# A fused graph-attention layer on one core: batch 0's self_feat by seven block products in the setup, partial sums in place

## The chip, the cores and the metric

The kernel runs on one core of a Trainium2 chip. The core has TensorE (matmuls, in the profile PE, and its weight loads PEld), VectorE (DVE), ScalarE (ACT), GpSimd (POOL) and SyncE (SP), which here only issues DMAs. Every engine works through its own instructions in order and waits on semaphores for the others. Matmuls write into PSUM, eight banks of 512 float32 for each of 128 partitions; VectorE and ScalarE read results from there. The metric is the device time in microseconds, as a median of several executions.

## What is computed

For 16 batches of 512 rows and 512 features (all float32):

```
q_exp     = 0 where a row of v sums to 0, else q[batch]
self_feat = concat(v, q_exp) @ W_self.T + b_self
output    = self_feat
for d in 0, 1:                       # both directions of the adjacency
    kv   = self_feat[:, :20]
    qh   = self_feat @ Wq[d].T + bq[d]          # 16 heads of 32
    kh   = kv @ Wk[d].T + bk[d]
    aff  = qh . kh / sqrt(32), masked by adj, plus a label bias
    out += softmax(aff) @ kv, each head through Wout[d], plus bout[d]
result    = v + relu(output)
```

The part that the change concerns is `self_feat`, a product of 512 x 512 by 512 x 512 for each batch, to which the q term is added (`nz`, the flags of rows that do not sum to zero, times `qw`, the q part of the product). The kernel holds it transposed: features on partitions, rows along the free dimension, in a tile `sf` of four chunks of 128 features. The first 20 rows (`NG`) come out of the setup already (`kvn`) and are copied in by `new_self`; the other 492 make two halves of 246 rows (`HN`).

## The kernel before, in words

There is a setup and a loop over batches with four tiles of 128 rows each (`nt`). All order is written out by hand (`manual_schedule`): instructions reach each engine's queue in the order of the program text.

**The setup** loads weights, computes the first 20 rows for all batches, and then works in 22 *bursts* (n = 0 to 21, function `keys`). A burst is eight matmuls into four PSUM banks (two tiles of the pool `ps_s`, which has just two), and these are copied out half by ScalarE (line 684) and half by VectorE (line 686) into a staging tile `st`, which SP then writes to DRAM for later batches. The next burst uses the same two tiles, so it has to wait for both copies. The stretch between two bursts is a *gap*. To fill gaps, the list `plan` names for each burst from n = 4 on what TensorE does behind it: `v` and `w` are steps of the value projection (`values`), `c` the bias scores, `n` the row flags of a batch (`row_flags`), and `s` a step of batch 0's self_feat (`self_step`: four matmuls). The fillers use four banks of the pool `ps_acc`.

**Batch 0's self_feat** is computed before in the plain way: `self_feat` runs for each pair of output chunks f and half h 32 matmuls of 32 output features and 236 or 256 rows, and `self_copy` adds the q term on VectorE on the way to `sf`. Three of the four (f, h) lie in gaps of the setup; the fourth, (1, 1), stands in the loop, at `nt == 1` of batch 0 between the first and the second tile's scores (line 864).

**From batch 1 on** self_feat is computed by seven block products instead of eight (a scheme of Strassen's kind, with four sums of weights, `weight_sums`, and four sums of x blocks for each batch, `x_sum`, both on GpSimd). `product(b, n)` is one of the seven: 16 matmuls with 246 columns. Products 1, 6, 7 and 4 accumulate one after the other into two banks `ps_a`; product 2 has the bank `ps_d`; products 5 and 3 accumulate in `ps_c`. Between the products VectorE takes out what stands in `ps_a` so far: `partial` adds the q term and writes a tile `u`, and `joined` adds a `u` to `ps_d` or `ps_c` and writes the block of `sf`. A product that adds to a bank has to wait until the `partial` or `joined` that reads the bank is through. These products for batch b + 1 run during batch b: products 1, 2 at its tile 2, 6, 7, 5 at its tile 3, and 4, 3 at tile 0 of batch b + 1.

**A tile of the loop**: `scores` (64 matmuls, line 353) into a `ps_s` tile, `weigh` on VectorE (add the mask `full`, which `full_add` makes on GpSimd; maximum; subtract), `expo` on ScalarE, `normal` (row sums on VectorE, scaling on GpSimd), `turn` (a transpose on VectorE). At tile 2 of the next batch, `attend` multiplies the weights with the value blocks `vd`, and `finish` and `residual` make the output. For batch 0 the value blocks are put together in DRAM by DMAs on SP (`clear_blocks`, `blocks`, `load_values`) during its own loop.

Of the kernel before, what the change touches and what calls it, by code (L numbers as in the profile page):

```python
# [13 lines left out]
P = 128  # L14
# [4 lines left out]
def gat_kernel(  # L19
# [71 lines left out]
    adds, fulls, wts, outs, held, sf_ps, conds, prods = {}, {}, {}, [], [None] * 3, {}, {}, {}  # L91
    sums, parts, us, done = {}, {}, {}, {}
# [98 lines left out]
    def self_feat(b, f, h, parts=((0, range(C)), (1, range(C)))):  # L191


        lo, hi = max(NG, h * N // 2), (h + 1) * N // 2
        for i, ks in parts:
            if (i, ks[0]) == (0, 0):
                if (f, h) == (0, 0):
                    new_self(b)
                held[0] = bank(f"ps_sf{b}_{f}{h}", 3 if (f, h) == (1, 1) else None)
            for k in ks:  # L200
                for a in range(HL):
                    nc.tensor.matmul(  # L202
                        held[0][bass.ts(a, R), i * N // 2 : i * N // 2 + hi - lo],
                        ws_v[:, k, bass.ds((2 * f + i) * P + a * R, R)], xs[b][:, k, lo:hi],
                        start=(k == 0), stop=(k == C - 1),
                    )
            if (i, ks[-1]) == (1, C - 1):
                sf_ps[b, f, h] = held[0]

    def self_copy(b, f, h):  # L210

        lo, hi = max(NG, h * N // 2), (h + 1) * N // 2
        ps = sf_ps.pop((b, f, h))
        for i in range(2):
            nc.vector.scalar_tensor_tensor(
                sfs[b][:, 2 * f + i, lo:hi], nzs[b][:, lo:hi], qw[:, 2 * f + i, b : b + 1],
                ps[:, i * N // 2 : i * N // 2 + hi - lo], ALU.mult, ALU.add,
            )

# [15 lines left out]
    def x_sum(b, n):  # L235

        t = sums[b, n] = xsum.tile([P, 2, HN], F32, tag=f"t{n}", name=f"t{b}_{n}")
# [8 lines left out]
    def product(b, n):  # L246
# [11 lines left out]
        if n == 1:  # L258
            parts[b, "a"] = [bank(f"ps_a{b}_{i}", i) for i in range(2)]
        if n == 2:  # L260
            parts[b, "d"] = bank(f"ps_d{b}", 2)
        if n == 5:
            parts[b, "c"] = bank(f"ps_c{b}", 3)
# [17 lines left out]
    def partial(b, n, f, l, to=None):  # L281

        if to is None:
            to = us[b, n] = xsum.tile([P, 2, HN], F32, tag=f"u{n}", name=f"u{b}_{n}")
        for i in range(2):
            done["partial"] = nc.vector.scalar_tensor_tensor(  # L286
                to[:, i], nzs[b][:, half(l)], qw[:, 2 * f + i, b : b + 1], parts[b, "a"][i][:, :HN],
                ALU.mult, ALU.add,
            )
# [4 lines left out]
    def joined(b, n, key, f, l):  # L294

        nc.vector.tensor_add(
            block(b, f, l), parts[b, key][:, : 2 * HN].rearrange("p (i n) -> p i n", i=2), us.pop((b, n))
# [155 lines left out]
    with tc.tile_pool(name="setup", bufs=1) as sp, tc.tile_pool(name="ps_acc", bufs=4, space=PSUM) as acc["pool"]:  # L453
# [157 lines left out]
        with tc.tile_pool(name="setup_g", bufs=4) as sg:  # L611
# [85 lines left out]
            def self_step(b, f, h, i, k):  # L697
                self_feat(b, f, h, ((i, (k,)),))
                if (i, k) == (1, C - 1):
                    self_copy(b, f, h)  # L700
# [6 lines left out]
                "s": [  # L707
                    (self_step, (0, f, h, i, k)) for f, h in ((0, 0), (1, 0), (0, 1))
                    for i in range(2) for k in range(C)
                ],  # L710
# [3 lines left out]
            plan = "bvv vv vv ccw vv ns ssss sssw vv vv ssss ssss vv vv nww ssss ssss".split()  # L714
# [13 lines left out]
            for n, runs in enumerate(bursts):  # L728
# [16 lines left out]
                if n == 10:  # L745
                    mask_sum(0, 0)
                    load_cq(0)
                if n == 11:
                    row_sums(1)
                if n == 13:  # L750
                    weight_sums()
# [17 lines left out]
    with tc.manual_schedule():  # L769
# [11 lines left out]
        for b in range(B):  # L781
# [7 lines left out]
            for nt in range(NT):  # L789
# [22 lines left out]
                if nt == 0:  # L812
# [4 lines left out]
                    else:  # L817
# [5 lines left out]
                        partial(b, 4, 1, 0, block(b, 1, 0))  # L823
# [222 lines left out]
```

## Time and profile before

| | us |
|---|---|
| median of three executions | 591.52 (590.48 to 591.87) |
| profiled execution, device time | 593.27 |
| its span, first to last instruction | 591.5 |
| TensorE busy | 578.7 |
| VectorE busy | 492.3 |
| ScalarE busy | 395.6 |
| GpSimd busy | 384.2 |
| mean granted TensorE clock | 0.995 |

The profile is one execution, recorded by the hardware. A line such as `L202 PE MATMUL ps_sf<-x,ws_v` names the line of the kernel, the engine, the operation, and the tile written and those read. In a timeline a line begins with the start in us from the first instruction and the duration; `xN` counts merged records (every matmul of this kernel leaves two). A bracket at the end says how long the engine stood idle just before and what ended that. The ends of matmuls are modelled: consecutive groups overlap by some 0.1 to 0.2 us, so the length of a group is read from its start to the start of the next.

### The profile page before, as it was taken

The page shows a single profiled execution, that of the slowest core. Times are in us where ns is not written, and L with a number is a line of the kernel's source. Part 1 is how long each engine was busy: PE and PEld are TensorE (multiplying, and loading weights), DVE is VectorE, ACT ScalarE, POOL GpSimd, SP SyncE. Part 2 cuts the span into 40 slices and gives each one's busy share as a digit, 9 for nine tenths or more (in the row PEclk, how much of TensorE's full clock was granted, in tenths as well). Part 3 has the DMA queues.
Part 4 walks back from the last instruction along what each step waited for, and adds up shares of the span by engine and source line. Part 5 has one row for each costly group of instructions (what it writes and reads, how often), then busy time and mean ns, then how long its engine had stood idle before and what let it go on. Part 6 is the DMA issues. An engine that isn't in the chain of part 4 may idle for free.

```text
span 591.5 us, 30038 instructions
## 1 busy us (share of the span) xinstructions
PE 578.7 (98%) x13180; PEld 439.7 (74%) x13180; DVE 492.3 (83%) x785; ACT 395.6 (67%) x1162; POOL 384.2 (65%) x351
## 2 busy tenths in 40 slices
PE   8999999999999999999999999999999999999994
PEld 6654547888978687787878787788787878787882
DVE  0495565889898888999999999888989898989896
ACT  1234644587877677768686868677787877777661
POOL 2315663638677675758686777675858677776774
PEclk9999999999999999999999999999999999999997
DMA  8998999857848485767676766757585748582503
GB/s 294 385 406 299 332 376 329 257 126 199 223 154 229 155 236 148 206 168 209 184 208 163 223 173 202 171 181 208 164 217 170 216 149 232 158 238 85 167 13 142
DMA packets 98129, 124.10 MB, mean 210 GB/s; under 512 B 19952, under 2 KB 70160, under 8 KB 95952
## 3 DMA queue, kind: packets, MB, share of 16 engines
q1 hardware_dynamic: 96752, 120.31, 67.1%
q8 instruction: 103, 1.69, 1.2%
q0 software_dynamic: 672, 1.36, 1.0%
q10 hardware_dynamic: 576, 0.53, 0.3%
q14 instruction: 26, 0.21, 0.1%
HBM read 82.30 MB, written 40.24 MB: 207 GB/s over the span
## 4 chain that ended last, share of the span: by engine, by line
PE 94%; DVE 3%; DMA 1%; issue 1%; ACT 0%; POOL 0%; SPq 0%; DVEq 0%; POOLq 0%; ACTq 0%
PE ps_s L353 44%; PE ps_a L279 17%; PE ps_c L279 8%; PE ps_o L426 6%; PE ps_d L279 4%; PE ps_v L644 3%; PE ps_k L581 3%; PE ps_sf L202 2%; DMA ws_q<-in_wsT 1%; PE ps_kv L532 1%; DVE o L435 0%; PE ps_nz L186 0%; DVE wt L415 0%; DVE ps_s L371 0%; DVE sm L406 0%
## 5 line engine op out<-in xcount | busy, mean ns | idle before, releaser
L353 PEld LDWEIGHTS ps_s<-g,sf 128*32 128x32 f32 x8192 | 264.0, 110 | 19.8 <-issue 12.2
L353 PE MATMUL ps_s<-g,sf 128*32 128x152 f32 x8192 | 277.3, 293 | 0.5 <-ACT st L684 0.5
L334 ACT COPY both<-add 32x80 f32<-32x80 f32 x512 | 130.9, 256 | 54.8 <-DVE add L325 49.0
L408 POOL TENSOR_TENSOR s<-s,sm 128x640 f32<-128x640 f32 x63 | 80.3, 1275 | 98.0 <-DVE sm L407 98.0
L341 POOL TENSOR_TENSOR full<-cq,both 128x640 f32<-128x640 f32 x64 | 100.1, 1565 | 30.3 <-issue 24.3
L314 ACT ACTIVATE prod<-adj,wb_sb 128x80 f32<-128x80 int32 x330 | 112.5, 432 | 0.0
L380 ACT ACTIVATE s<-s 128x640 f32<-128x640 f32 x63 | 46.5, 738 | 69.4 <-DVE s L375 69.0
L444 POOL TENSOR_TENSOR o<-o,x 128x512 f32<-128x512 f32 x60 | 75.9, 1285 | 0.0
L367 DVE TENSOR_TENSOR full<-ps_s,full 128x608 f32<-128x608 f32 x63 | 49.1, 779 | 32.1 <-PE ps_s L353 26.6
L406 DVE TENSOR_REDUCE sm<-s 128x32 f32<-128x640 f32 x63 | 50.9, 808 | 8.8 <-ACT s L380 8.6
L279 PE MATMUL ps_a<-t,ws_s 128*32 128x246 f32 x960 | 55.5, 370 | 0.0
L371 DVE TENSOR_REDUCE ps_s<-full 128x32 f32<-128x640 f32 x63 | 52.2, 828 | 2.2
L415 DVE STREAM_TRANSPOSE wt<-s 128x640 f32<-128x640 f32 x63 | 52.8, 839 | 0.1
L375 DVE TENSOR_TENSOR s<-full,ps_s 128x640 f32<-128x640 f32 x63 | 51.6, 818 | 1.1
L426 PE MATMUL ps_o<-wt,vd 32*32 32x512 f32 (+5 forms) x816 | 40.8, 581 | 3.7 <-DVE wt L400 2.0
L279 PEld LDWEIGHTS ps_a<-t,ws_s 128*32 128x32 f32 x960 | 32.2, 110 | 15.5
L325 DVE TENSOR_REDUCE add<-prod 128x80 f32<-128x960 f32 x32 | 36.8, 1150 | 6.3 <-ACT prod L314 4.4
L244 POOL TENSOR_TENSOR t<-x 128x492 f32<-128x492 f32 x30 | 34.4, 1148 | 10.1 <-DVE full L367 5.2
L439 ACT ACTIVATE o<-o,bo 128x512 f32<-128x512 f32 x60 | 38.2, 708 | 0.6 <-POOL biased L881 0.6
L435 DVE TENSOR_TENSOR o<-ps_o,sf 128x512 f32<-128x512 f32 x60 | 36.8, 672 | 1.0 <-PE ps_o L426 1.0
L286 DVE SCALAR_TENSOR_TENSOR u<-nz,qw,ps_a 128x246 f32<-128x246 f32 x90 | 36.6, 449 | 0.0
L244 POOL TENSOR_TENSOR t<-x,t 128x492 f32<-128x492 f32 x30 | 34.4, 1147 | 1.2
(238 smaller groups left out, 722.7 us busy)
## 6 DMA issues: line engine op xcount, KB each, us to landing
g_d<-st SPq DMA_DIRECT2D x16, 1064.0 KB, 5.9
g<-g_d SPq DMA_DIRECT2D x28, 608.0 KB, 5.2
out_T<-o SPq DMA_DIRECT2D x60, 256.0 KB, 4.7
xn<-in_xn SPq DMA_DIRECT2D x28, 512.0 KB, 3.6
x<-in_xT SPq DMA_DIRECT2D x28, 512.0 KB, 4.3
adj<-in_adj SPq DMA_DIRECT2D x32, 440.0 KB, 5.0
nz<-nz_d SPq DMA_DIRECT2D x14, 256.0 KB, 4.0
wk<-in_wkT SPq DMA_DIRECT2D x2, 1024.0 KB, 8.0
```

Of the source, the lines that this page charges most:

```text
L244: nc.gpsimd.tensor_sub(t, one, two)
L279: nc.tensor.matmul(to, lhs, x[:, k], start=start, stop=stop, skip_group_check=n != 2)
L314: nc.scalar.activation(p[:, :, l], a[:, :, l], AF.Identity, scale=wb_sb[:, l : l + 1])
L334: nc.scalar.copy(adds[b, h][bass.ts(a, R), :, g], add[r].rearrange("p (t m) -> p t m", t=2))
L341: nc.gpsimd.tensor_add(f, cqs[b].unsqueeze(1).to_broadcast(shape), adds[b, nt // 2][:, nt % 2].unsqueeze(2).to_broadcast(shape),)
L353: nc.tensor.matmul(bank[bass.ts(a, R), bass.ts(j, WD // HL)], sfs[b][:, k, bass.ds(nt * P + (2 * g + j) * R, R)], keys[:, k, a], start=(k ...
L371: nc.vector.tensor_reduce(mx, f, AX.X, ALU.max)
L375: nc.vector.tensor_sub(s, f, mx.unsqueeze(3).to_broadcast(full))
L408: done["normal"] = nc.gpsimd.tensor_mul(s, s, sm.unsqueeze(3).to_broadcast(full))
L415: nc.vector.transpose(wts[b][:, nt], s.rearrange("p a h m -> p (a h m)"))
L426: nc.tensor.matmul(banks[a][bass.ds(at // 2 * DH, n * DH)].rearrange("p (t n) -> p t n", n=32), vd[r, bass.ds(at * DH, n * DH)], wt[r, :, ...
L444: nc.gpsimd.tensor_add(o[:, c], o[:, c], xs[b][:, c])
```

## The change

Batch 0 gets its self_feat by the seven block products too.

- `self_feat` and `self_copy` are gone, and with them the 96 matmuls in gaps and the 32 matmuls in the loop at tile 1 of batch 0.
- The last seven gaps (n = 14 to 20) get one product each, in the order 1, 2, 6, 7, 5, 4, 3. Ahead of a product in the same gap stand, on VectorE: a partial ahead of 2, 7 and 4, a join ahead of 6 and 3; behind product 3 the last partial and the last join.
- The other fillers move up into n = 4 to 13; `row_sums(1)` and `weight_sums` move to n = 9, and at n = 11 the four x sums of batch 0 are made on GpSimd, into a tile of the `sf` pool.
- For all batches the partials are written straight into the block of `sf` and the join adds in place; the tiles `u` are gone. So `new_self` of the next batch moves from tile 3 to tile 2, ahead of that tile's exponential on ScalarE.
- In the setup the banks of the products come from the setup's own pool of four.

```diff
@@ x_sum
-        t = sums[b, n] = xsum.tile([P, 2, HN], F32, tag=f"t{n}", name=f"t{b}_{n}")
+        if b > 0:
+            t = xsum.tile([P, 2, HN], F32, tag=f"t{n}", name=f"t{b}_{n}")
+        else:
+            if n == 1:
+                held[0] = sfp.tile([P, C, N], F32, tag="sf", name="t0")
+            t = held[0][:, n - 1, : 2 * HN].rearrange("p (k n) -> p k n", k=2)
+        sums[b, n] = t
@@ product
-            parts[b, "a"] = [bank(f"ps_a{b}_{i}", i) for i in range(2)]
+            parts[b, "a"] = [bank(f"ps_a{b}_{i}", i if b else None) for i in range(2)]
...
@@ partial, joined
-    def partial(b, n, f, l, to=None):
-        if to is None:
-            to = us[b, n] = xsum.tile([P, 2, HN], F32, tag=f"u{n}", name=f"u{b}_{n}")
+    def partial(b, f, l):
+        to = block(b, f, l)
...
-    def joined(b, n, key, f, l):
+    def joined(b, key, f, l):
         nc.vector.tensor_add(
-            block(b, f, l), parts[b, key][:, : 2 * HN].rearrange("p (i n) -> p i n", i=2), us.pop((b, n))
+            block(b, f, l), parts[b, key][:, : 2 * HN].rearrange("p (i n) -> p i n", i=2), block(b, f, l)
         )
@@ the setup's fillers
-            def self_step(b, f, h, i, k):
-                self_feat(b, f, h, ((i, (k,)),))
-                if (i, k) == (1, C - 1):
-                    self_copy(b, f, h)
+            def block_product(n):
+                first = {
+                    2: (partial, (0, 0, 0)), 6: (joined, (0, "d", 0, 0)), 7: (partial, (0, 0, 1)),
+                    4: (partial, (0, 1, 1)), 3: (joined, (0, "c", 1, 1)),
+                }
+                if n in first:
+                    f, args = first[n]
+                    f(*args)
+                product(0, n)
+                if n == 3:
+                    partial(0, 1, 0)
+                    joined(0, "c", 0, 1)
...
+                "p": [(block_product, (n,)) for n in (1, 2, 6, 7, 5, 4, 3)],
...
-            plan = "bvv vv vv ccw vv ns ssss sssw vv vv ssss ssss vv vv nww ssss ssss".split()
+            plan = "bvv vvc vvc vvn vv vvw vv vv ww wn p p p p p p p".split()
@@ beside the bursts
+                if n == 9:
+                    row_sums(1)
+                    weight_sums()
                 if n == 11:
-                    row_sums(1)
-                if n == 13:
-                    weight_sums()
+                    new_self(0)
+                    for i in range(1, 5):
+                        x_sum(0, i)
@@ the loop, nt == 1
-                    if b == 0:
-                        self_feat(0, 1, 1)
                     for g in range(2):
                         scores(b, nt, g, ps[g])
-                    if b == 0:
-                        self_copy(0, 1, 1)
@@ the loop, nt == 2
-                    s = weigh(b, nt, pair, (lambda: partial(b + 1, 1, 0, 0)) if more else None)
+                        new_self(b + 1)
+                    s = weigh(b, nt, pair, (lambda: partial(b + 1, 0, 0)) if more else None)
@@ the loop, nt == 3
-                    new_self(b + 1)
-                    joined(b + 1, 1, "d", 0, 0)
+                    joined(b + 1, "d", 0, 0)
```

46 lines of the change are left out of this document (9 added, 37 removed).

## The prediction

> **What bounds the kernel now.** I read the page first: busy time, then the chain that ended last, to learn which engine's time is the kernel's time.
>
> ```profile
> span 591.5 us, 30038 instructions
> PE 578.7 (98%) x13180; PEld 439.7 (74%) x13180; DVE 492.3 (83%) x785; ACT 395.6 (67%) x1162; POOL 384.2 (65%) x351
> PE 94%; DVE 3%; DMA 1%; issue 1%; ACT 0%; POOL 0%; SPq 0%; DVEq 0%; POOLq 0%; ACTq 0%
> ```
>
> TensorE is busy 98% of the span and holds 94% of the chain. Every microsecond of matmuls removed is gained, and every microsecond for which TensorE is made to wait is lost. So I next asked for the busy time by stretch: the setup with its key bursts, batch 0's 32 self_feat matmuls inside the loop, and the batches from batch 1's second half on.
>
> ```profile
> 43.53:91.46 47.93, 47.93 (x513) 23.26 (x513) 28.46 (x50) 22.77 (x53) 28.67 (x34) 1.00 0.93 336
> 96.68:100.13 3.45, 3.45 (x72) 2.08 (x64) 2.44 (x3) 0.47 (x1) 1.05 (x1) 1.00 1.05 313
> 133.53:560.00 426.47, 425.07 (x10812) 336.77 (x10812) 385.46 (x595) 322.07 (x969) 306.20 (x265) 1.00 0.67 188
> ```
>
> The columns are the stretch, its length, then busy time of PE, PEld, DVE, ACT, POOL, granted clock, DMA share, GB/s. In the setup stretch TensorE never stands still: 47.93 of 47.93 us. The timeline of one gap shows how it manages that.
>
> ```profile
> 78.96 0.40 PE L669 MATMUL ps_g(3, 0, 1, 1, 2)0_786<-khD,wq_sb 32*128 32x152 f32 x2
> 79.95 1.98 PE L644 MATMUL ps_v<-wo_sb,kvT 128*128 128x512 f32 x4
> 80.11 1.17 DVE L686 TENSOR_SCALAR st<-ps_g(3, 0, 1, 1, 2)1_787 128x304 f32<-128x304 f32 x2 [0.69 <-PE ps_g(3, 0, 1, 1, 2)1_787 L669]
> 81.86 0.53 PE L669 MATMUL ps_g(3, 1, 1, 0, 2)0_809<-khD,wq_sb 32*128 32x304 f32 x2
> ```
>
> A burst of keys takes 0.98 us (78.96 to 79.95). VectorE then needs until 81.28 to copy it out, and the next burst needs those banks. In between TensorE runs a filler of 1.91 us that waits for nobody. A gap therefore costs the filler's length, as long as the filler can start at once and is longer than about 1.4 us.
>
> **The change, part by part.** *Matmuls.* Removed are 96 matmuls of batch 0's self_feat in the gaps and 32 in the loop; added are 7 products of 16 matmuls, all in gaps.
>
> ```profile
> 71.62 1.80 PE L202 MATMUL ps_sf<-x,ws_v 128*32 128x236 f32 x32
> 73.35 0.40 PE L669 MATMUL ps_g(2, 3, 0, 1, 2)0_727<-khD,wq_sb 32*128 32x152 f32 x2
> 86.75 1.93 PE L202 MATMUL ps_sf<-x,ws_v 128*32 128x256 f32 x32
> 88.61 0.53 PE L669 MATMUL ps_g(3, 3, 0, 0, 2)0_875<-khD,wq_sb 32*128 32x304 f32 x2
> 118.47 1.88 PE L279 MATMUL ps_a<-t,ws_s 128*32 128x246 f32 x32
> 120.13 1.87 PE L279 MATMUL ps_c<-t,ws_s 128*32 128x246 f32 x32
> ```
>
> Sixteen matmuls of 236 columns fill a gap for 1.73 us (71.62 to 73.35), of 256 columns for 1.86. So one of 246 columns takes 1.80 in a gap; it is 1.66 between other matmuls (118.47 to 120.13). Seven products in gaps: 12.6 us. Removed from the gaps: four fillers' worth at 1.73, two at 1.86, and 0.14 because one of them was spread over three gaps: 10.8. Net +1.8 in the setup. The 32 matmuls in the loop save 3.45 (96.68 to 100.13). With nothing else the change would gain 1.65.
>
> *New waits in the gaps.* This is the part that I expect to decide. The products accumulate into two shared banks (ps_a). A partial copies them out between two products, and the plan puts the partial and the next product in the same gap, the partial first. On VectorE it is queued behind the copy of that gap's keys; on TensorE the product waits for it, and the next burst waits behind the product. Product 7 waits so for partial (0,1), product 4 for partial (1,1), product 3 for the join of block (1,1), which reads the bank that product 3 adds to. Products 1, 2 and 5 open fresh banks; product 6 waits for a partial issued one gap earlier and long done.
>
> ```profile
> 63.55 1.16 DVE L686 TENSOR_SCALAR st<-ps_g(2, 0, 0, 1, 2)1_595 128x304 f32<-128x304 f32 x2
> 64.63 0.82 DVE L215 SCALAR_TENSOR_TENSOR sf<-nz,qw,ps_sf 128x236 f32<-128x236 f32 x2
> 64.86 0.53 PE L669 MATMUL ps_g(2, 1, 0, 0, 2)1_636<-khD,wq_sb 32*128 32x304 f32 x2
> 113.71 0.66 DVE L296 TENSOR_TENSOR sf<-ps_d,u 128x492 f32<-128x492 f32 x1
> ```
>
> Count from the moment at which the filler could start. The copy runs from 0.16 to 1.33 (79.95 against 80.11 and 1.17). The partial starts 0.08 before the copy's recorded end (64.63 against 64.71), at 1.25, and the first of its two halves (0.82 for both) is over by about 1.70. TensorE follows 0.15 after VectorE's end (64.71 to 64.86): the product starts at 1.85. The join (0.66) instead ends at 1.91, so product 3 starts at 2.05. Nothing else stands in TensorE's queue for that time. Waits: 1.85 + 1.85 + 2.05 = 5.75 us. Bounds: 0 if these copies were somehow done before the keys end, and 2.4 each if both halves of a partial were waited for, so 0 to 7.
>
> *What the new order removes.* The rows above also show VectorE late in the old plan: its copy began only at 63.55, and the second half of the next burst waited for it. Twice a burst took 1.4 us and not 0.98. In the new plan the reduction and copies that made it late fall in gaps where VectorE has time: -0.85 (0 if they recur).
>
> *The steps that move.* Value, flag and bias-score fillers only change gaps. The first bias score now comes two gaps earlier, and its ScalarE copy waits for a memset on GpSimd that stands behind a DMA issue there:
>
> ```profile
> 48.52 0.66 POOL L623 MEMSET c<- 128x640 f32 x1
> 63.88 2.62 POOL L182 TENSOR_TENSOR rx<-rx,x 128x512 f32<-128x512 f32 x2
> 72.58 1.28 POOL L224 TENSOR_TENSOR ws_s<-ws_v 128x512 f32<-128x512 f32 x1
> L244 POOL TENSOR_TENSOR t<-x,t 128x492 f32<-128x492 f32 x30 | 34.4, 1147 | 1.2
> ```
>
> The memset ends at 49.2 in both plans; the ScalarE copy of the next keys falls in behind it and ends just after its gap: +0.15 (0 to 1). GpSimd's line before product 6 grows by four x sums: from about 62 us it has batch 1's row sums (3 x 1.31), the weight sums (4 x 1.28), a DMA issue of 0.8 and the x sums (4 x 1.15), done near 76.5. Product 6's turn is near 79.5, so this costs nothing; each microsecond beyond 79.5 would hold TensorE. SP's order is unchanged. Setup in all: 1.8 + 5.75 - 0.85 + 0.15 = +6.85.
>
> *The loop's start.* Call the start of batch 0's scores S (92.52 before).
>
> ```profile
> 92.52 4.34 PE L353 MATMUL ps_s<-g,sf 128*32 128x152 f32 x128 [0.52 <-ACT st L684]
> 100.13 8.45 PE L353 MATMUL ps_s<-g,sf 128*32 128x152 f32 x256
> 108.40 1.84 PE L279 MATMUL ps_a<-x,ws_v 128*32 128x246 f32 x32
> 111.43 1.45 PE L279 MATMUL ps_d<-x,ws_v 128*32 128x246 f32 x24 [0.77 <-issue]
> 133.53 2.24 PE L426 MATMUL ps_o<-wt,vd 32*32 32x512 f32 x48
> 101.78 1.27 POOL L408 TENSOR_TENSOR s<-s,sm 128x640 f32<-128x640 f32 x1 [2.61 <-DVE sm L407]
> 105.31 1.56 POOL L341 TENSOR_TENSOR full<-cq,both 128x640 f32<-128x640 f32 x1
> 109.01 0.73 DVE L367 TENSOR_TENSOR full<-ps_s,full 128x608 f32<-128x608 f32 x1
> 110.51 0.84 DVE L286 SCALAR_TENSOR_TENSOR u<-nz,qw,ps_a 128x246 f32<-128x246 f32 x2
> L136 SPq DMA_DIRECT2D vd<-bd_d x4: 336/423/1149, 126.2 to 128.3; - x4
> DMA to landing us min/median/max: 1.9/2.6/2.8
> ```
>
> Without the 3.45 us, the three score tiles run back to back and product 1 of batch 1 starts at S + 12.4, not S + 15.9. What does not come earlier is the softmax of tile 0: GpSimd's line from its normalisation (101.78) to the end of the third sum for the mask (105.31 + 1.56) still ends at S + 14.35. VectorE's add for tile 2 waits for that; its partial starts 1.5 later (109.01 to 110.51), frees the bank at about S + 16.4, and product 6 starts at S + 16.55 where its turn is S + 15.75: 0.8 lost. Before, product 2 stood still for 0.77 for no reason that the trace names. If that stays, it hides my 0.8; if it goes, it pays for it: I count both together as 0 (-0.77 to +0.8). Next late: the loads of batch 0's value blocks. Their DMAs hang on SP's own line after S, which nothing shortens, and the last lands at the latest at about S + 38.6 (last issue at 128.3, up to 2.8 to its landing, 131.1). The attention product now wants it at about S + 37.6, against S + 41.0. I take +0.5 (0 to 1). Loop: -3.45 + 0.5 = -2.95.
>
> *In place instead of u, batches 1 to 15.* The instructions are the same in number and size, and VectorE has 41 us of slack in the 426 us stretch above. The block's ScalarE copy moves ahead of an exponential that has been waiting for VectorE anyway:
>
> ```profile
> 238.30 0.74 ACT L380 ACTIVATE s<-s 128x640 f32<-128x640 f32 x1 [1.86 <-DVE s L375]
> 238.94 0.24 ACT L302 COPY sf<-kvn 128x80 f32<-128x80 f32 x1
> ```
>
> 0.24 in front of 1.86 of idle time: 0. Were that cover gone, it would be 15 x 0.24 = 3.6 at most.
>
> **Sum.** +6.85 - 2.95 = +3.9 us. The profiled execution took 593.27 us, its span 591.5 and 1.77 around it; that is 1.75 above the median of 591.52, and I carry the difference over to the median: **595.4 us**, 0.66% slower. By the bounds, its own range is 593 to 597.5.
>
> **The rivals.** *The waits aren't there (faster).* Place: products 7, 4 and 3. If their banks were free when the keys end, the sum is 3.9 - 5.75 = -1.85: **589.7 us**. It becomes faster once the three waits together cost under 1.85, that is 0.6 each. For it: TensorE in the setup is never idle now. Against it: no filler now needs a bank that a copy of the same gap frees, and VectorE's 1.17 us copy comes first in all of its gaps. 8%. *They half cancel (same).* Waits near 0.6 each, or a faster start of the loop: 591.5. 6%. *The loop's gain is lost.* If the value loads or VectorE's line hold the loop to its old times, only the setup counts: +6.85, **598.4 us**. For it is the 0.8 and the 1.0 worked out above; against it that TensorE, not VectorE, paces the stretch (33.4 us from 100.13 to 133.53 with one idle of 0.77). 8%. *The clock falls.* A gap with such a wait leaves TensorE idle for 1.85 of some 4.6 us, three times within 15 us. At the kernel's end there is one idle time of this length:
>
> ```profile
> 582.87:584.85 1.98, 0.00 (x2) 0.00 (x1) 1.88 (x5) 0.34 (x1) 1.94 (x2) 1.00 0.35 132
> 585.48:586.02 0.54, 0.54 (x16) 0.14 (x9) 0.24 (x2) 0.00 (x0) 0.00 (x0) 0.50 0.00 0
> ```
>
> After 1.98 us of idle the granted clock reads 0.50 within another 0.7 us, with small matmuls running. If each of the three products ran at half clock, they would take 1.66 us more each: +5, **600.4 us**. Against it: the idle here is shorter, and full-size matmuls follow. 16%. The Trainium skill (TensorE: Matmul & The Clock Gate, Part 1) says that the clock halves after at least one idle window of about 3.4 us; by that rule these waits are too short and the time stays at the forecast. The row at 585.48 agrees only if the window is not fully idle, so the measurement leaves the door open.
>
> **How the numbers follow.** Forecast 62%, clock 16%, loop's gain lost 8%, waits absent 8%, half cancelled 6%. The forecast's own 593 to 597.5, stretched upwards over the lost loop gain and the milder half of the clock case and downwards by half a microsecond, gives 592.5 to 599.5, with under two in ten left out. A change of 0.2% (1.2 us) is about what can be told from none. Slower: 62 + 16 + 8 = 86%; same 6%; faster 8%.
>
> **What would show it.** In the changed profile, TensorE should be idle before product 7, 4 and 3 in the gaps, each with VectorE's copy out of ps_a or ps_c as releaser, 1.85, 1.85 and 2.05 us. Batch 0's first scores should start near 99.4, and the attention product near 137.4. The granted clock should stay 1.00 in the setup. Batches from there on should take as long as now. I am wrong if those three idle times are below 0.6 us, if the clock reads 0.50 there, or if the batches from 1 on have grown.

## The result, and the profile after

The changed kernel takes **597.54 us** in the median of six runs (593.96 to 599.56), the kernel before 591.30 (590.36 to 592.32): a ratio of 1.0102, 95% interval 1.0071 to 1.0133. It is 1% slower; 595.4 was forecast.

The page of the changed kernel, its busy time and the chain that ended last:

```profile
span 596.3 us, 29980 instructions
PE 575.7 (97%) x13148; PEld 439.4 (74%) x13148; DVE 493.3 (83%) x788; ACT 395.3 (66%) x1162; POOL 388.6 (65%) x355
PE 79%; DVE 3%; issue 2%; ACT 0%; POOL 0%; DVEq 0%; POOLq 0%; ACTq 0%
```

TensorE is busy for 3.0 us less than before (578.7) in a span that is 4.8 us longer. So it stands idle for 7.8 us more. Where it does so, and where it runs slower, is shown by its busy time in stretches, first of the kernel before, then of the changed one. The columns are the stretch, its length, busy time and count for PE, PEld, DVE, ACT and POOL, granted clock, DMA share, GB/s.

```profile
43.53:92.52 48.99, 48.47 (x521) 23.57 (x521) 29.38 (x53) 23.21 (x54) 29.73 (x34) 1.00 0.93 337
92.52:133.53 41.01, 40.24 (x1057) 35.31 (x1057) 31.35 (x48) 25.87 (x84) 18.61 (x19) 1.00 0.79 228
133.53:579.97 446.44, 444.74 (x11293) 352.27 (x11289) 404.14 (x623) 333.96 (x997) 320.93 (x277) 1.00 0.64 181
```

```profile
41.33:97.22 55.89, 49.84 (x553) 24.43 (x552) 32.19 (x58) 23.21 (x54) 34.54 (x38) 1.00 0.86 308
97.22:140.10 42.88, 38.87 (x992) 37.76 (x992) 30.71 (x46) 25.82 (x84) 19.25 (x19) 0.96 0.78 222
140.10:584.84 444.74, 443.05 (x11290) 349.37 (x11288) 403.42 (x623) 333.73 (x997) 319.93 (x276) 1.00 0.62 181
```

The three stretches are the setup from the burst at n=5 to batch 0's first scores, the loop's start from there to the first attention product, and the other batches. The setup grew by 6.90 us. The loop's start grew by 1.87, and its clock reads 0.96. The batches took 1.70 less. The changed kernel's n=5 burst began 2.20 earlier (41.33 against 43.53), in code that the change leaves alone; in the twelve profiles of this case's kernels without added matmuls ahead of it, this point lies between 41.3 and 44.4, so that is scatter between executions. With 0.07 less at the end, 6.90 + 1.87 - 1.70 - 2.20 - 0.07 gives the 4.8 us.

In the setup's timeline TensorE now waits three times. The columns are start, duration, instruction, count, and in brackets the idle time before it and its releaser.

```profile
80.23 1.17 DVE L662 TENSOR_SCALAR st<-ps_g(3, 0, 1, 1, 2)1_793 128x304 f32<-128x304 f32 x2
81.32 0.84 DVE L262 SCALAR_TENSOR_TENSOR sf<-nz,qw,ps_a 128x246 f32<-128x246 f32 x2
81.93 2.07 PE L256 MATMUL ps_a<-t,ws_s 128*32 128x246 f32 x32 [1.79 <-DVE sf L262]
89.56 1.87 PE L256 MATMUL ps_a<-t,ws_v 128*32 128x246 f32 x32 [1.79 <-POOL g L669]
94.37 1.87 PE L256 MATMUL ps_c<-x,ws_s 128*32 128x246 f32 x32 [1.96 <-DVE sf L272]
```

Products 7, 4 and 3 stand behind VectorE's copy of the gap's keys (80.23) and then behind the partial (81.32) that frees their bank: 1.79, 1.79 and 1.96 us. (At product 4 the row names GpSimd. But VectorE's partial of that gap starts at 88.95, and the product 0.61 later, as product 7 does after the partial at 81.32; so it was that.)

The loop's start holds what was not forecast. Its timeline, and two of its stretches:

```profile
97.22 6.67 PE L329 MATMUL ps_s<-g,sf 128*32 128x152 f32 x200 [0.52 <-ACT st L660]
105.73 4.33 PE L329 MATMUL ps_s<-g,sf 128*32 128x152 f32 x127 [1.84 <-issue]
112.24 2.94 PE L329 MATMUL ps_s<-g,sf 128*32 128x152 f32 x57 [2.17 <-issue]
```

```profile
110.07:112.24 2.17, 0.00 (x2) 0.00 (x1) 2.09 (x4) 1.82 (x5) 1.50 (x1) 1.00 1.06 373
113.33:116.74 3.41, 3.41 (x52) 3.26 (x45) 1.42 (x2) 1.58 (x6) 1.98 (x2) 0.50 0.98 371
```

TensorE stops twice in the middle of a run of equal score matmuls, for 1.84 and 2.17 us, and "issue" says that the profile knows nothing that it waits for. Then the clock is 0.50 for 3.41 us of uninterrupted work, which loses half of that, 1.7 us. The loop's start adds up: 3.45 saved, 4.01 of such idle time instead of 0.77, and 1.7 for the clock are +1.5 of the 1.87.

What the two idle times have in common is their distance: 128 records (one of them is missing in the trace, so the row says 127). TensorE executes 13148 matmul and 13148 weight-load records; the page's DMA queues show what brings them.

```profile
q8 instruction: 103, 1.69, 1.2%
```

103 packets for 26296 records are 255 to a packet: 128 matmul records and their 128 weight loads, 16 KB. Call such a packet's instructions a piece, and the place in the stream where one ends an edge. Counted from the first matmul, the idle times stand ahead of records 964 and 1092, and the one idle time "issue" of the kernel before (0.77, in product 2) ahead of record 1220. All three leave 68 when divided by 128. The DMA view of four short windows of the changed kernel (queue and kind: packets, MB, share of 16 engines):

```profile
q1 hardware_dynamic: 1086, 1.68, 57.0%
...
q1 hardware_dynamic: 723, 0.44, 109.4%
q8 instruction: 1, 0.02, 4.9%
...
q1 hardware_dynamic: 2054, 1.92, 109.8%
...
q1 hardware_dynamic: 391, 0.40, 103.0%
q8 instruction: 1, 0.02, 5.3%
```

The windows are 93.7 to 103.2, 103.2 to 104.5, 104.5 to 109.9 and 109.9 to 111 us. No packet of instructions starts in the first window. One starts at 103.31, just before TensorE stops (103.89), and takes 1.02; matmuls resume 1.40 us after its landing. The next starts at 109.97 (TensorE stops at 110.07), takes 0.93, and matmuls resume 1.34 us after it. Both come in full DMA engines (share over 100%). That gave the theory for the experiments: **TensorE's instructions come in pieces of 16 KB through the same DMA engines as the data, and where these are loaded a piece comes late.** A piece lasts 4.1 us in the scores (of the kernel before, 256 records from 100.13 to 108.40) and 6.6 in products (32 records in 1.66), so the scores are where it shows.

The two profiles show the lateness itself. Around batch 0's scores a packet starts only after TensorE has passed the edge before the one that it is needed for. In the changed kernel the two packets start 3.74 and 4.24 us after TensorE passed records 836 (99.57) and 964 (105.73). In the kernel before, those behind records 836, 964 and 1092 start 1.19, 0.68 and 3.40 us after them, and only the third stops TensorE: it lands at 109.99, and matmuls resume at 111.43. With 1.0 for the transfer and 1.4 to resume, a start later than about 1.7 us after the edge stops TensorE in the scores (4.1 - 1.0 - 1.4, an estimate from these figures). A full share alone does not make a packet late: in the kernel before it is 1.05 and 1.09 in 96.9 to 98.2 and 101.9 to 103.4, where the two early ones come. What decides about a packet's turn among the transfers is not shown. (Product 7 in the setup starts at an edge too, record 580, but its packet had landed 4.9 us before, so its wait is not of this kind.)

### The profile page after: what moved, and what is told of

It reads as the page before. It is cut to its first block, busy times and chain, and to the rows that moved or that the text cites. A ratio compares the mean times of both kernels' runs of the same rounds, so it can differ in the third digit from the quotient of the medians.

```text
span 596.3 us, 29980 instructions
## 1 busy us (share of the span) xinstructions
PE 575.7 (97%) x13148; PEld 439.4 (74%) x13148; DVE 493.3 (83%) x788; ACT 395.3 (66%) x1162; POOL 388.6 (65%) x355
## 4 chain that ended last, share of the span: by engine, by line
PE 79%; DVE 3%; issue 2%; ACT 0%; POOL 0%; DVEq 0%; POOLq 0%; ACTq 0%
PE ps_s L329 44%; PE ps_a L256 17%; PE ps_c L256 9%; PE ps_o L402 6%; PE ps_d L256 4%; DVE o L411 0%; DVE wt L391 0%; DVE ps_s L347 0%; DVE sm L382 0%; DVE full L343 0%; POOL s L384 0%; DVE st L662 0%; DVE s L373 0%; DVE sm L371 0%; DVE s L351 0%
## 5 line engine op out<-in xcount | busy, mean ns | idle before, releaser
L256 PE MATMUL ps_a<-t,ws_s 128*32 128x246 f32 x1024 | 59.5, 371 | 1.8 <-DVE sf L262 1.8
L262 DVE SCALAR_TENSOR_TENSOR sf<-nz,qw,ps_a 128x246 f32<-128x246 f32 x128 | 51.5, 442 | 0.6 <-PE ps_a L256 0.6
L256 PEld LDWEIGHTS ps_a<-t,ws_s 128*32 128x32 f32 x1024 | 34.6, 110 | 18.5 <-POOL g L669 2.2
L221 POOL TENSOR_TENSOR t<-x 128x492 f32<-128x492 f32 x32 | 36.7, 1148 | 10.9 <-DVE full L343 7.2
L402 PE MATMUL ps_o<-wt,vd 32*32 32x512 f32 (+5 forms) x816 | 38.1, 579 | 2.3 <-DVE wt L376 2.0
L221 POOL TENSOR_TENSOR t<-x,t 128x492 f32<-128x492 f32 x32 | 36.7, 1146 | 1.3
```

Source lines behind the costliest of these rows:

```text
L221: nc.gpsimd.tensor_sub(t, one, two)
L256: nc.tensor.matmul(to, lhs, x[:, k], start=start, stop=stop, skip_group_check=n != 2)
L262: done["partial"] = nc.vector.scalar_tensor_tensor(to[:, i], nzs[b][:, half(l)], qw[:, 2 * f + i, b : b + 1], parts[b, "a"][i][:, :HN], AL ...
L402: nc.tensor.matmul(banks[a][bass.ds(at // 2 * DH, n * DH)].rearrange("p (t n) -> p t n", n=32), vd[r, bass.ds(at * DH, n * DH)], wt[r, :, ...
```

## The experiments

Each ratio is to the kernel before, run on the same chip beside it. It is not the quotient of the two medians and differs from that by up to 0.002.

| kernel | median, us | before | ratio, 95% interval |
|---|---|---|---|
| changed kernel | 597.54 | 591.30 | 1.0102 (1.0071 to 1.0133) |
| behind_products | 592.12 | 593.63 | 0.9968 (0.9951 to 0.9985) |
| quiet_loads | 603.95 | 593.63 | 1.0190 (1.0152 to 1.0228) |
| work_put_back | 603.03 | 593.63 | 1.0161 (1.0135 to 1.0186) |
| in_place_alone | 593.42 | 593.63 | 1.0006 (0.9990 to 1.0022) |
| join_earlier | 596.01 | 592.93 | 1.0054 (1.0040 to 1.0067) |
| calm_loads | 595.94 | 592.93 | 1.0050 (1.0030 to 1.0069) |
| loop_short | 589.23 | 592.93 | 0.9946 (0.9927 to 0.9965) |
| extra_zeros | 597.97 | 592.93 | 1.0088 (1.0072 to 1.0105) |
| later_rows | 602.00 | 592.71 | 1.0163 (1.0149 to 1.0177) |
| later_rows_keys | 600.90 | 592.71 | 1.0156 (1.0128 to 1.0184) |
| edges_32 | 594.98 | 593.27 | 1.0026 (1.0006 to 1.0046) |
| edges_96 | 594.11 | 593.27 | 1.0012 (0.9996 to 1.0029) |

### The three waits: behind_products

```diff
-                first = {
-                    2: (partial, (0, 0, 0)), 6: (joined, (0, "d", 0, 0)), 7: (partial, (0, 0, 1)),
-                    4: (partial, (0, 1, 1)), 3: (joined, (0, "c", 1, 1)),
-                }
-                if n in first:
-                    f, args = first[n]
-                    f(*args)
+                behind_it = {
+                    1: (partial, (0, 0, 0)), 2: (joined, (0, "d", 0, 0)), 6: (partial, (0, 0, 1)),
+                    7: (partial, (0, 1, 1)), 5: (joined, (0, "c", 1, 1)), 4: (partial, (0, 1, 0)),
+                    3: (joined, (0, "c", 0, 1)),
+                }
                 product(0, n)
-                if n == 3:
-                    partial(0, 1, 0)
-                    joined(0, "c", 0, 1)
+                f, args = behind_it[n]
+                f(*args)
```

> The changed kernel, but each copy out of a product's bank (the partials and joins of batch 0) is put right behind the product that fills the bank, ahead of the next burst's copies, and no longer in the next gap. Theory (the three waits are VectorE's queue, nothing else): the idle times of 1.79, 1.79 and 1.96 us before products 7, 4 and 3 go, the span from the burst at n=5 to batch 0's first scores falls from 55.9 to some 50.4 us, and the time from 597.5 to 592.0 us. Rival (the gaps are full anyway: with the waits gone the bursts wait for VectorE's late copies or for the stores of the keys): half or less of it, 594.5 us or more. The idle times inside batch 0's scores stay in both.

Its stretches, setup and loop's start, and then two rows of its timeline:

```profile
43.11:93.08 49.97, 49.45 (x554) 23.96 (x553) 32.54 (x58) 23.21 (x54) 34.06 (x38) 1.00 0.90 323
93.08:132.94 39.86, 37.37 (x992) 33.07 (x992) 30.36 (x46) 26.03 (x84) 17.92 (x18) 1.00 0.79 229
```

```profile
90.22 1.87 PE L256 MATMUL ps_c<-x,ws_s 128*32 128x246 f32 x32
...
104.87 2.02 PE L329 MATMUL ps_s<-g,sf 128*32 128x152 f32 x56 [1.00 <-issue]
```

Product 3 (90.22) has no idle time before it, nor have 7 and 4. The setup falls from 55.89 to 49.97, 0.4 below what was expected, and is 0.98 longer than before the change. The copies were only in the wrong place of VectorE's queue: behind the product that fills the bank they run while TensorE does the next burst. This kernel is faster than both, 0.9968 of the kernel before. Against the changed kernel that is 0.0134, or 7.9 us, more than the 5.5 of the waits: the loop's start too is 3.0 shorter (39.86 against 42.88), with less idle time at the edges and a clock of 1.00.

### In place: in_place_alone

The kernel before with `to = block(b, f, l)` in partial, the join from block to block, and new_self(b + 1) behind product 2.

> The kernel before with only the second part of the change: the partial sums of batches 1 to 15 written into self_feat's blocks, and the block's copy on ScalarE ahead of the exponential. Forecast: no difference, 591.3 us (within 0.5). Rival (the copy of 0.24 us is not hidden, 15 times): 594.9 us.

1.0006, 0.4 us, with an interval of 0.9 either way. The 0.24 us copies are hidden; 3.6 us is ruled out.

### Late instructions: where the idle times stand

*work_put_back* puts 32 matmuls of 256 columns back ahead of batch 0's second score tile.

```diff
+                    if b == 0:
+                        spare = bank("ps_x", 0)
+                        for i in range(2):
+                            for k in range(C):
+                                for a in range(HL):
+                                    nc.tensor.matmul(
+                                        spare[bass.ts(a, R), i * N // 2 : (i + 1) * N // 2],
+                                        ws_v[:, k, bass.ds((2 + i) * P + a * R, R)], xs[0][:, k, N // 2 :],
...
                     for g in range(2):
                         scores(b, nt, g, ps[g])
```

> The changed kernel with 32 matmuls of 256 columns put back into the loop, between batch 0's first and second score tile, where self_feat had them; their result goes to a bank that nobody reads. Theory (late instructions): they give the instruction loads time, most of the 4.0 us of idle time and the half clock go, and the 3.45 us of added work cost little: 596 to 598 us. Rival (the loop is simply TensorE's work plus unrelated idle times): 597.5 + 3.45 = 601 us.

It came out as the rival has it: 1.0161, 3.5 us above the changed kernel. The time alone would speak against the theory. Its profile says why, in the timeline and in two stretches of the setup's end:

```profile
109.04 4.56 PE L329 MATMUL ps_s<-g,sf 128*32 128x152 f32 x135
115.50 4.17 PE L329 MATMUL ps_s<-g,sf 128*32 128x152 f32 x121 [1.90 <-issue]
```

```profile
93.65:95.61 1.96, 0.01 (x2) 0.00 (x1) 1.80 (x4) 1.00 (x2) 0.50 (x2) 1.00 0.36 139
96.57:103.39 6.82, 6.30 (x90) 3.94 (x86) 2.21 (x3) 2.48 (x9) 0.37 (x1) 0.50 0.46 146
```

The first idle time is gone. The second (1.90) stands ahead of score record 264 (128 before the added work, then 136), no longer 328 (the row of 135 has one record missing). With the 64 added records it is the same place of the stream: record 1092. But after product 3's wait of 1.96 us (93.65 to 95.61) the clock is 0.50 for 6.82 us. In the changed kernel's profile the same wait left it at 1.00. What differs is said in the last section.

*edges_32* and *edges_96* shift the stream on purpose, on behind_products: small matmuls at the kernel's first, where TensorE waits for weights (in edges_96 they stand for three of the seven first ones).

```diff
             for _ in range(7):
                 nc.tensor.matmul(warm[:, :P], ones, ones, start=True, stop=True)
+            for _ in range(16):
+                nc.tensor.matmul(warm[:32, :32], ones[:, :32], ones[:, :32], start=True, stop=True)
```

> The kernel with the copies right behind the products, and 16 small matmuls (32 by 32, 32 records in the trace; their result is not read) behind the first ones of the kernel, where TensorE waits for weights. Nothing else moves, but every later instruction stands 32 records further on in TensorE's stream. Theory (idle times stand at the ends of 16 KB pieces of the stream): in batch 0's scores they come only ahead of records 40, 168 or 296 of the 384, no longer at 328, and the one that stood in product 6 comes 32 records earlier. Rival (they belong to a place of the program): again ahead of record 328 and in product 6. The time is not foretold better than the ratio 0.990 to 1.000.

> The same with 51 small matmuls in place of three of the seven first ones: 96 records more in the stream. Theory: idle times in batch 0's scores only ahead of records 104, 232 or 360; the last of them is followed by the products of batch 1, whose 128 records take 6 us and not 4.1, so that at most two idle times are left and the ratio is 0.992 to 0.997. Rival: again ahead of record 328 and in product 6, 0.997.

The timeline of edges_32, then of edges_96:

```profile
93.82 9.77 PE L329 MATMUL ps_s<-g,sf 128*32 128x152 f32 x296 [0.52 <-ACT st L662]
105.19 3.05 PE L329 MATMUL ps_s<-g,sf 128*32 128x152 f32 x88 [1.60 <-issue]
...
112.48 1.45 PE L256 MATMUL ps_d<-x,ws_v 128*32 128x246 f32 x24 [2.17 <-issue]
```

```profile
94.32 11.83 PE L329 MATMUL ps_s<-g,sf 128*32 128x152 f32 x360 [0.52 <-ACT st L662]
107.22 0.98 PE L329 MATMUL ps_s<-g,sf 128*32 128x152 f32 x24 [1.07 <-issue]
...
114.12 4.20 PE L329 MATMUL ps_s<-g,sf 128*32 128x152 f32 x122 [0.68 <-issue]
```

The idle times went to score records 296 and 360, and the ones after them lie 128 further on in the stream. None stands at 328. No wait of the program moves with a count of matmuls that nothing reads, so this part of the theory is **shown**: the idle times stand at the edges of the 16 KB pieces. The ratio that was expected for edges_96 (0.992 to 0.997) was missed: the shift gained nothing (1.0026 and 1.0012), and against behind_products it cost 3.4 and 2.6 us. The small matmuls were not free. The first matmul on loaded weights begins at 6.2 and 7.3 us instead of 4.5, and batch 0's scores come 0.7 and 1.2 us later than in behind_products. That is within the scatter of this point between executions, and the rest of the cost is open.

### Late instructions: what makes them late

*quiet_loads* moves the loop's first transfers, *calm_loads* tries it again on behind_products, with the zeros earlier (n=15) and batch 1's second mask half ahead of the value blocks.

```diff
+                if n == 20:
+                    clear_blocks(zero)
...
-        load_keys(1)
...
                     load_adj(1, 0)
                     load_cq(1)
-                    clear_blocks(zero)
-                    load_adj(1, 1)
-                    load_xn(2, 0)
-                    load_xn(2, 1)
                 if b == 0 and nt == 2:
+                    load_keys(1, range(C), done["exp"])
+                    load_xn(2, 0)
+                    load_xn(2, 1)
                     blocks()
+                    load_adj(1, 1)
```

> The changed kernel with the transfers of the loop's start moved out of batch 0's first three score tiles: the 2 MB of zeros into the last burst's gap, batch 1's keys and batch 2's rows behind the second exponential, batch 1's second mask half behind the value blocks. Theory (TensorE stands still inside batch 0's scores because its own instructions come late on the loaded DMA engines): the idle times of 1.84 and 2.17 us go, and with them the stretch at half clock (about 1.7 us): 592 us, up to 594 if a moved transfer comes late. Rival (the idle times have another cause, in TensorE or in a wait that the profile does not name): they stay, 597.5 us.

> The kernel with the copies right behind the products (ratio 0.9968), and the transfers of the loop's start moved: the zeros into the setup at n=15, batch 1's keys, second mask half and batch 2's rows behind the second tile's exponential. In batch 0's first two score tiles only some 0.5 MB are loaded. Theory (TensorE's instructions come in pieces of 16 KB, 128 matmuls each, and come late behind other transfers): no idle time inside batch 0's scores at the piece's edge, instead of 1.00 and 1.49 us: ratio 0.993. Rival (the edge itself costs, whatever the load): idle times at every edge or the same two, 0.997. A new wait for a moved transfer would show with its releaser and is neither.

Both missed in time. Of quiet_loads the timeline, one stretch, and one row of the waits (total, times, longest):

```profile
108.00 6.15 PE L329 MATMUL ps_s<-g,sf 128*32 128x152 f32 x184 [1.58 <-issue]
```

```profile
108.00:112.50 4.50, 4.50 (x140) 4.50 (x144) 3.12 (x5) 1.69 (x7) 3.50 (x3) 1.00 0.02 4
```

```profile
PE ps_c L256 <- DVE sf L272: 8.7, 2, 6.8
```

Until 106 us the engines were as full as ever, now with the zeros, and the first idle time stayed (1.58). From 108.0 to 112.5 they were empty (share 0.02), and TensorE went through record 1092, where the changed kernel stops for 2.17, without a pause. So late packets do matter at that edge: this one started 1.04 us after the edge before it. But the mask half that was moved last made TensorE wait 6.8 us for VectorE's join, and then the clock read 0.50 for 10.24 us. calm_loads was not calm either: the zeros, put among the stores of the keys, pushed them past the setup's end; it had idle times of 0.21 and 1.61, and GpSimd started its sums only at 105.4, which cost TensorE 3.25.

*extra_zeros* asks the other way round: 2.1 MB more in each of four batches of the kernel before, which nobody waits for.

```diff
+                if nt == 0 and 5 <= b < 9:
+                    nc.sync.dma_start(spare_d[b - 5], zero.unsqueeze(1).to_broadcast([P, 16, HL * 2 * DH]))
```

> The kernel before with 2.1 MB of zeros more, written at the start of each of batches 5 to 8 to memory that nobody reads. No instruction waits for them. Theory (late instructions): TensorE, which takes 30.48 us for a batch, stands still in these batches for 1 to 3 us each where a piece of 128 matmuls ends, with no releaser named: ratio 1.007 to 1.02. Rival (TensorE is bound by its matmuls; a write that nobody waits for is free): ratio 1.000. If the batch's own loads come late instead, the idle time has a releaser (a DMA or VectorE) and is neither.

1.0088: 5.2 us for 8.4 MB. The stretch from attention product to attention product where it shows most, in the kernel before and then with the zeros:

```profile
319.85:350.53 30.68, 30.68 (x788) 24.43 (x784) 27.87 (x43) 23.52 (x71) 22.18 (x20) 1.00 0.67 191
```

```profile
320.89:353.37 32.48, 31.45 (x786) 26.89 (x785) 28.07 (x43) 23.61 (x71) 23.73 (x21) 1.00 0.80 247
```

The work is the same; DMA share rises from 0.67 to 0.80, and the stretch takes 1.80 longer at full clock. The time is within what the theory expected; the idle times are not, for it expected 1 to 3 us in each of the four batches. In the profile the four stretches in which zeros are written are 0.20, 0.10, 0.84 and 1.80 us longer than the same ones of the kernel before, and the idle times without a releaser add up to 2.2 us. So a loaded DMA engine is a risk, not a fixed price.

*loop_short* takes 24 of the 32 matmuls out of the loop of the kernel before: `self_feat(0, 1, 1, ((0, (0,)), (1, (0,))))`.

> The kernel before; of batch 0's 32 self_feat matmuls in the loop it computes 8 and leaves out 24 (three quarters of the sum for block (1,1)). By the forecast's own rule these 24 are 2.6 us of work on the path: 593.6 - 2.6 = 591.0, ratio 0.9956. Theory (late instructions): without them TensorE reaches the edges of its pieces sooner than the loaded DMA engines bring the next, and idle times of 1 to 2 us come in the scores: ratio 0.998 to 1.000, with the idle time of 0.7 us of the kernel before grown to 2 us or more. Rival (the idle times of the changed kernel come from its setup): the idle time stays at 0.7 us, ratio 0.9956.

The theory's number fell. 0.9946 is 3.2 us, and the 2.6 of plain arithmetic (0.9956) lies in its interval. The one idle time in its first scores, and product 6 of batch 1:

```profile
103.77 1.50 PE L353 MATMUL ps_s<-g,sf 128*32 128x152 f32 x40 [0.21 <-issue]
...
108.38 2.32 PE L279 MATMUL ps_a<-t,ws_s 128*32 128x246 f32 x31
```

Less work in the loop does not by itself bring idle times: there the edges lie 32 records later in the scores than in the changed kernel (104, not 72), because that kernel's setup has 32 records more. So what the change met is the meeting of three things: where the edges lie, the scores behind them, and the transfers of that moment. Product 6 (108.38) does not wait for VectorE. The prediction had foreseen 0.8 there for a loop without the 32 matmuls.

*later_rows* moves only batch 1's second mask half and batch 2's rows behind the value blocks, *later_rows_keys* also batch 1's keys behind the second exponential; both on behind_products.

```diff
-                    load_adj(1, 1)
-                    load_xn(2, 0)
-                    load_xn(2, 1)
                 if b == 0 and nt == 2:
                     blocks()
+                    load_adj(1, 1)
+                    load_xn(2, 0)
+                    load_xn(2, 1)
```

> The kernel with the copies right behind the products, and 1.5 MB of the loop's start (batch 1's second mask half and batch 2's rows, with the row sums that read them) moved behind the value blocks' writes; batch 1's keys and the zeros stay where they were. Theory (TensorE's instructions come late behind other transfers): the second idle time at a piece's edge (1.49 us, its piece fetched while mask half, rows and zeros were being moved) goes or shrinks below 0.7, the first (1.00 us, its piece fetched beside the keys) stays: ratio 0.9945, against 0.9968. Rival (it is the sum of the transfers that counts, the zeros alone fill the engines): both stay, 0.9968.

> As the kernel before it, and batch 1's keys wait for the second tile's exponential too. Theory: the first idle time (1.00 us) shrinks as well, since beside that piece only 0.5 MB and the zeros are moved: ratio 0.993 to 0.994. Rival (the zeros, now in the keys' place, hold the piece as the keys did): it stays, 0.9945 to 0.997. A wait of GpSimd or of the attention product for a moved transfer would show with its releaser and is neither.

The second idle time did shrink, from 1.49 to 0.74, in later_rows; the first stayed (1.25). In later_rows_keys there are 1.62 and 1.34 at the edges at 964 and 1092, so there the theory missed in this too. Against behind_products the time went up by some 11 us in both. The waits of later_rows, of all engines, at the loop's start:

```profile
ACT xn L166 <- DMA xn<-in_xn: 8.2, 2, 7.8
...
PE ps_o L402 <- issue: 4.2, 1, 4.2
DVE cond L295 <- DMA adj<-in_adj: 3.9, 1, 3.9
...
PE ps_c L256 <- DVE sf L272: 2.4, 1, 2.4
```

VectorE's mask counts and ScalarE's row sums stand at the head of their queues for 3.9 and 7.8 us, and the attention product comes 7.9 us later than in behind_products, after 4.2 us of idle time for which the profile names no releaser. The loads of the loop's start are in a good order for those who read them; I found none that also keeps the edges free.

### The clock: join_earlier

Block (1,1) is joined right behind its partial, in the gap of product 4 instead of product 3's.

```diff
+                if n == 4:
+                    joined(0, "c", 1, 1)
                 product(0, n)
```

> The changed kernel with one join moved: block (1,1) of batch 0 is joined one gap earlier, right after its partial, so that product 3 (idle before it: 1.96 us) waits for nothing; the two waits of 1.79 us stay. Theory (the clock): only an idle time that fills more than about 1.9 us of one 3.41 us window of the clock halves the clock in the next window; product 3's 1.96 us does so in some of the runs, by where the windows fall, the 1.79 us never. So the wait's 1.96 us go and with them 1.7 to 3.4 us in about half of the runs: ratio to the kernel before 1.0102 - 0.0033 - 0.003 = 1.004, and the mean granted clocks of nearly all runs are 0.994 to 0.997 instead of 0.990 to 0.996. Rival (the clock falls for idle times inside the scores alone): 1.0069, the clocks as scattered as now.

1.0054 is 2.8 us below the changed kernel, where the wait itself is 1.96. The interval ends just short of the rival's 1.0069, but that number rests on the changed kernel's 1.0102, which is itself known only to 0.003: the time does not decide. The mean clocks are still scattered (0.992 to 0.997), which the theory denied. How much of the changed kernel's scatter is product 3's wait stays open. Its profile has a whole clock and gives the loop's start without that loss (the stretch, then a row of its timeline):

```profile
96.53:136.75 40.22, 37.58 (x993) 34.29 (x993) 30.73 (x46) 26.00 (x84) 18.02 (x18) 1.00 0.78 220
```

```profile
104.90 4.34 PE L329 MATMUL ps_s<-g,sf 128*32 128x152 f32 x128 [1.70 <-issue]
```

## Why the prediction was right, and where it was wrong

The sign and the range held: 597.54 in 592.5 to 599.5. The number was 2.1 us too low. That the range held is in part luck: the forecast's own range ended at 597.5, and the rest was added for two rivals that did not come as they were put.

- *The waits in the gaps* (1.85, 1.85, 2.05, sum 5.75): right. 1.79, 1.79 and 1.96, sum 5.54, behind the two VectorE instructions named, and gone when these are moved. The setup is then 5.92 shorter.
- *The rest of the setup* (+1.8 of matmuls, -0.85, +0.15): right in sum. Without the waits the setup is 0.98 longer, 1.10 was forecast. In all +6.90 against +6.85.
- *The loop's start, -2.95*: wrong, and this is the step that failed. The 3.45 of removed work did go; it was given back. The prediction saw the 0.77 us of "issue" in product 2, "no reason that the trace names", and set it off against product 6's wait as 0 (-0.77 to +0.8). It was the trace's sign of a mechanism whose size depends on the place in the instruction stream: 2.63 us of such idle time in join_earlier's profile, 4.01 in the changed kernel's. The loop's start gained 0.8 in the one (40.22 against 41.01) and lost 1.87 in the other, with 1.7 of it for the clock. With the first, 6.90 - 0.8 = 6.1 is the measured difference of 6.2; that this profile stands for the median is an argument, not shown.
- *Product 6's wait, 0.8*: in no run. VectorE is through with the first half of its partial at S + 16.4, as forecast (behind_products, edges_96 and loop_short), but TensorE, which was to be there at S + 15.75, comes at S + 16.95 at the earliest (behind_products), after its idle time at an edge. With TensorE on time the wait is untested.
- *The value loads, +0.5*: not seen. In behind_products the attention product begins at 132.94, 39.9 us after the scores, and in loop_short 38.5 us after them, with no wait. S + 37.6, for which the wait was forecast, was not reached.
- *In place, 0*: right, 0.4 within 0.9.
- *The rival that the clock falls*: it does, but not as put. In the changed kernel's profile it fell not in the gaps but after the 2.17 us at an edge, for 3.41 us; in work_put_back after product 3's wait, for 6.82. "Loop's gain lost", 598.4, came nearest in the number, and by neither of the two causes it named.

## What to carry to other kernels

Put the copy that frees a bank behind the matmuls that fill it, not in front of the matmuls that need it: on an in-order engine these differ by whatever is queued between them, here three times 1.8 us. An idle time that the profile puts down to "issue", inside a run of equal instructions, is worth counting: if such places are a fixed number of instructions apart, look for the packets of the instruction queue. Here they were late instruction loads, and their price changed with the transfers of that moment and with everything that shifted the stream. When work is taken out of a stretch where the DMA engines are full, don't book all of it as gain without looking where the edges then fall: here 3.45 us of work gained nothing in one kernel, and 2.6 us gained in full in another (loop_short).

## What the runs showed of the hardware that I had not expected

- TensorE's instructions came in packets of 16 KB (103 for 26296 records), each asked for about one piece ahead, and a late one stopped TensorE for 0.2 to 2.2 us at edges 128 matmul records apart under a DMA share near 1; at a share of 0.02 the same edge cost nothing. Matmuls resumed some 1.4 us after the packet had landed. The Trainium skill (Runtime: NRT & Kernel Launch, Instruction fetch mechanics) gives the same size of a block, 16 KiB or 256 instructions, and says that crossing its boundary is mostly hidden. The size agrees. "Hidden" holds in the setup of behind_products, where pieces last 6.2 to 7.5 us and no idle time stands at an edge; it does not hold in the scores.
- The clock went to 0.50 after idle times of 1.96 us (work_put_back) and 2.17 (changed kernel), not after 1.79 or 1.84, and not after the changed kernel's 1.96 or the 2.17 of edges_32. It stayed there for 3.41 us, 6.82, and 10.24 in quiet_loads. Its changes lie multiples of 3.41 us apart: the changed kernel's clock is 1.00 for 109.23 us, 32 times 3.41. Counted in such windows, TensorE was idle for 57% of the one before the drop in work_put_back (93.15 to 96.57) and for 64% in the changed kernel (109.91 to 113.33). It was idle for 54% of 103.09 to 106.50, which holds the 1.84 us, and the clock stayed; the changed kernel's 1.96 us and the 2.17 us of edges_32 are each split over two windows, and fill 45% and 48% of one at most. In the fourteen profiles every window at full clock with 57% or more idle is followed by 0.50, and none with 55% or less. The Trainium skill (TensorE: Matmul & The Clock Gate, Part 1) has a free-running window of 3413 ns, which these lengths fit, and asks for a whole idle window, which they contradict: a window filled a little over half was enough.
- Runs of one kernel scatter by up to 5 us (the kernel before, 23 runs on one chip: 591.50 to 596.49). From attention product to attention product half of the batches or more take 30.48 us in both kernels' profiles, and some up to 32.05; whether those too are late pieces wasn't tested.
